# Reordering the work around a convolution in a hybrid layer: next inputs begun earlier, products by turns, residuals at set times, weight sums on another engine

## Chip, cores and metric

One core of one Trainium2 chip. The metric is the device time of the core in microseconds (us); lower is better. The kernel before took 3203.71 us (median of 4 runs).

## The reference

Two layers on x of 4 x 128 x 64 x 64 (four images, 128 channels on the 128 partitions, 4096 pixels), all in float32. The change touches layer 0 only:

```python
def _L0_conv_ref(x, w7, b7, w5, b5, w3, b3, gw, gb, tw, tb, pw, pb, ow, ob):
    x7 = conv2d(x, w7, b7, 3)
    x5 = conv2d(x, w5, b5, 2)
    x3 = conv2d(x, w3, b3, 1)
    xn = nonlocal_block(x, gw, gb, tw, tb, pw, pb, ow, ob)   # softmax attention over the 4096 pixels
    return jax.nn.relu(x7 + x5 + x3 + xn + x)

x = x + _L0_conv_ref(_gn(x), ...)                            # layer 0
# layer 1: a two-way state-space model, then a recurrence, both over the same 4 x 4096 tokens (not touched)
```

## The kernel before

The three convolutions are summed into one 7x7 kernel and done in a transformed (Winograd-like) form: eight products m = 0 to 7 for an image, each with its own transformed input rows ("forms", made on GpSimd) and its own transformed weights (made in turn 0, kept in DRAM, fetched when wanted). The products m = 6, 7 are light (two groups of input, no weights to fetch), m = 1 to 4 have three groups, m = 0, 5 have five. Attention of an image has eight query blocks of 512. So an image is eight *turns*, each of one attention part (scores on TensorE, exp on ScalarE, values on TensorE, the softmax sum `es` on VectorE) and one product; layer 0 has 32 turns, n = 0 to 31. The results of m = 1 to 4 go to four phases of the image rows, so m = 2 and m = 4 leave scaled additions, the *residuals*, to be done in the attention part of a later turn.

```python
# cuts are marked ...
def products(f, kxs):
    pm = ps_c.tile([P, 2, KB // 2 * PC], F32, tag="c", name="pm")     # ring of THREE PSUM tiles, tag "c"
    ...
def put_middle(n, u, v, at):                                          # residuals of m = 2, 4
    spare = lambda: wk.tile([P, 2, KB // 2 * PC], F32, tag="xr", name="sc")        # two tiles
    later(lambda: put(n, 2, u, at * at, spare() if (b, n, 2) in begun else None))  # ScalarE mul, GpSimd add
    later(lambda: put(n, 1, in_(v), at, spare() if (b, n, 1) in begun else None))
    later(lambda: put(n, 3, in_(v), at * at * at, v))
def divide(n, acc, es):
    den = ps_c.tile([P, NC], F32, tag="c", name="den")                # from the same ring
    nc.tensor.matmul(den, k.ones, es[:, 0, :], start=True, stop=True)
    nc.vector.reciprocal(att, den)
    ...
    nc.vector.tensor_tensor(att, acc, att, ALU.mult)
def collect(n, att):                                                  # attention result into the image t
    pc = ps_c.tile([P, NC], F32, tag="c", name="pc")
    nc.tensor.matmul(pc, ow, att, start=True, stop=True)
    nc.vector.tensor_tensor(r, r, pc, ALU.add)
# in weights(): the sums of the kernels, and the "thirds"
nc.gpsimd.tensor_tensor(w[:, z0:z1, 2:5, :], w[:, z0:z1, 2:5, :], w3[:, z0 - 2 : z1 - 2], ALU.add)
nc.gpsimd.tensor_tensor(ac, v[0], v[2], ALU.add)
nc.gpsimd.tensor_tensor(new, ac, v[1], ALU.subtract)
nc.gpsimd.tensor_tensor(v[1], ac, v[1], ALU.add)
# the store of a set of weights
nc.gpsimd.tensor_tensor(both, *own, ALU.add)

FIRST = (6, 7, 1, 2, 0, 5, 3, 4)      # image 0
ORDER = (1, 2, 0, 6, 7, 5, 3, 4)      # images 1, 2
LAST  = (1, 2, 3, 4, 6, 7, 5, 0)      # image 3
for n in range(N):
    b, q = divmod(n, NQ)
    m = (FIRST if b == 0 else ORDER if b + 1 < B else LAST)[q]
    making_forms = forms(m, f)                       # inputs of THIS turn's product
    next(making_forms, None)
    for i in range(NB):                              # attention, 8 pieces
        exs = nxt
        if i + 1 < NB: nxt = scores(th, i + 1)
        values(i, exs, acc, es)
        next(making_forms, None)
        next(making, None)                           # weights, in the first turns
        if m < 6 and i == NB - 3: wts = [fetch(m, 0), fetch(m, 1)]
        if late: late.pop(0)()                       # one residual a piece, as soon as there is one
    for i, _ in enumerate(convolve(b, m, f, wts)):   # half products: first, second, first, ...
        if i == 0:
            ...collects...
            if q == 0 and n: finish(b - 1)           # relu and residual of the whole image b - 1, late too
            atts[n] = divide(n, acc, es)
        if i == 2 and n + 1 < N: th = queries(n + 1) # from the ring "c" as well
    if n + 1 < N: nxt = scores(th, 0)
```

The order of instructions on TensorE and ScalarE is the program's; on VectorE and GpSimd a scheduler sets it at build time. In the traces each engine takes its instructions in that order: in turn 4 of this kernel exp stands behind a residual for which ScalarE waits 14.71 us.

## Time and profile before

| | before |
|---|---|
| median, us | 3203.71 |
| span of the profiled run | 3197.6 |
| to the first values matmul | 39.6 |
| 31 turns (values of turn 0 to values of turn 31) | 1626.4 |
| the rest (turn 31, state-space model, recurrence) | 1531.6 |
| turns 0 / 4 / 8 / 16 / 24 | 77.2 / 74.9 / 58.6 / 59.9 / 59.0 |

A turn's length is read from TensorE's timeline: from its first values matmul to the next turn's.

### The profile page before, as it was taken

The numbers are of one execution on the slowest core, as the hardware profiler recorded it, in microseconds if no ns is written. First come the engines' busy times: TensorE is split into PE (matmuls) and PEld (weight loads), VectorE is DVE, ScalarE is ACT, GpSimd is POOL, SyncE is SP. The second block draws the span as 40 slices with busy tenths as digits, with TensorE's granted clock in tenths as the row PEclk, the third lists the DMA queues.
The fourth block names the chain that finished last, engine by engine and source line by source line (L and its number), as shares of the span: only waits on it lengthen the run. The fifth ranks groups of instructions, "written<-read, shape, count | busy, mean of one in ns | idle before, by whom it ended". The sixth has DMA issues, their size and how long they took to land. (4 is left out here: it accounts for less than half of the span.)

```text
span 3197.6 us, 42890 instructions
## 1 busy us (share of the span) xinstructions
PE 2953.9 (92%) x15511; PEld 1463.8 (46%) x15511; DVE 2263.5 (71%) x3408; ACT 1817.2 (57%) x3102; POOL 1875.5 (59%) x1415
## 2 busy tenths in 40 slices
PE   5798998999989999999997899999999999999986
PEld 1344443445444544344454454544444444444545
DVE  5885676866867677677765676768676767677667
ACT  2343434433435334443443887887788778888756
POOL 6175757825768347677464355556655665555554
PEclk9999999999999999999998899999999999999988
DMA  4310010100111000111003333333433343333332
GB/s 166 144 38 30 23 45 29 62 4 23 38 37 57 8 23 23 38 56 45 1 23 113 93 105 107 91 97 83 116 97 93 91 112 95 97 101 94 88 114 107
DMA packets 108394, 224.16 MB, mean 70 GB/s; under 512 B 25678, under 2 KB 29390, under 8 KB 106764
## 3 DMA queue, kind: packets, MB, share of 16 engines
q1 hardware_dynamic: 96588, 177.53, 19.2%
q10 hardware_dynamic: 11584, 43.78, 3.9%
q8 instruction: 125, 2.05, 0.3%
q14 instruction: 97, 0.79, 0.1%
HBM read 200.83 MB, written 20.44 MB: 69 GB/s over the span
## 5 line engine op out<-in xcount | busy, mean ns | idle before, releaser
L475 DVE TENSOR_TENSOR es<-es,ex 128x1024 f32<-128x1024 f32 x448 | 767.3, 1713 | 121.6 <-ACT ex L460 82.5
L460 ACT ACTIVATE ex<-pf 128x1024 f32<-128x1024 f32 x512 | 502.0, 1023 | 436.9 <-PE pf L458 356.4
L458 PE MATMUL pf<-theta,phi 64*128 64x512 f32 x2048 | 517.9, 623 | 46.0 <-ACT ex L460 44.5
L469 PE MATMUL acc<-ex,gT 128*64 128x512 f32 x2048 | 492.2, 606 | 2.1 <-ACT ex L460 2.1
L1189 POOL TENSOR_TENSOR ct<-ct,Cst 128x512 f32<-128x512 f32 x128 | 169.7, 1326 | 393.1 <-DMA ct<-csmem 332.9
L458 PEld LDWEIGHTS pf<-theta,phi 64*128 64x128 f32 x2048 | 172.8, 187 | 369.8 <-ACT ex L460 226.3
L408 ACT ACTIVATE eo<-pm 128x256 f32<-128x256 f32 x88 | 33.7, 383 | 491.0 <-PE pm L366 491.0
L1155 ACT ACTIVATE lt<-lt,cs 128x128 f32<-128x128 f32 x1024 | 312.1, 390 | 0.3 <-DMA lt<-csmem 0.3
L366 PE MATMUL pm<-yf,wt 128*128 128x256 f32 x1152 | 294.5, 389 | 17.3 <-DVE t L491 12.9
L469 PEld LDWEIGHTS acc<-ex,gT 128*64 128x64 f32 x2048 | 127.6, 137 | 341.0 <-issue 329.4
L366 PEld LDWEIGHTS pm<-yf,wt 128*128 128x128 f32 x1152 | 217.1, 193 | 95.2 <-issue 40.8
L337 POOL TENSOR_TENSOR yf<-yd 128x272 f32<-128x272 f32 x192 | 242.0, 1291 | 0.0
L1090 PE MATMUL pb<-tl,wbc_fwd 128*64 128x512 f32 x512 | 234.9, 602 | 3.2 <-DVE xT L1122 3.2
L1090 PE MATMUL pb<-tl,wbc_bwd 128*64 128x512 f32 x512 | 235.5, 602 | 0.0
L424 POOL TENSOR_TENSOR eo<-eo 128x512 f32<-128x512 f32 x48 | 63.2, 1316 | 271.2 <-DVE eo L418 188.6
L1254 POOL TENSOR_TENSOR yT<-yT,zT 128x512 f32<-128x512 f32 x127 | 171.1, 1355 | 36.9 <-DVE yT L1241 32.4
L1188 DVE TENSOR_TENSOR lt<-lt,gm 128x1024 f32<-128x1024 f32 x128 | 179.7, 1404 | 1.9
L387 POOL TENSOR_TENSOR t<-t,eo 128x512 f32<-128x512 f32 x36 | 50.2, 1394 | 202.5 <-DVE eo L416 201.2
L337 POOL TENSOR_TENSOR yf<-yx 128x272 f32<-128x272 f32 x96 | 151.3, 1604 | 1.6
L1122 DVE SCALAR_TENSOR_TENSOR xT<-px,taps_bwd,xT 128x512 f32<-128x512 f32 x192 | 143.8, 749 | 8.9 <-ACT xT L1116 4.0
L1221 PE MATMUL y<-lt,xdt 128*64 128x128 f32 x2048 | 142.8, 282 | 4.1 <-PE ptr L1164 3.7
L412 DVE SCALAR_TENSOR_TENSOR eo<-pm,eo 128x256 f32<-128x256 f32 x176 | 73.6, 418 | 100.2 <-ACT eo L408 98.1
(297 smaller groups left out, 5792.7 us busy)
## 6 DMA issues: line engine op xcount, KB each, us to landing
lt<-csmem SPq DMA_DIRECT2D x128, 512.0 KB, 5.6
wt<-wd ACTq DMA_DIRECT2D x72, 576.0 KB, 3.7
ct<-csmem SPq DMA_DIRECT2D x256, 128.0 KB, 5.2
rs<-m SPq DMA_DIRECT2D x31, 512.0 KB, 3.6
wd<-t SPq DMA_DIRECT2D x16, 576.0 KB, 3.8
t<-in_x SPq DMA_DIRECT2D x4, 2048.0 KB, 10.9
rows<-after SPq DMA_DIRECT2D x32, 256.0 KB, 4.9
out<-t SPq DMA_DIRECT2D x4, 2048.0 KB, 14.4
```

The source lines that it names most:

```text
L337: nc.gpsimd.tensor_tensor(f[:, kx], at(x), at(y), op)
L366: nc.tensor.matmul(pm[:, e, :], wt, src, start=(i == 0), stop=(i == len(terms) - 1))
L458: nc.tensor.matmul(pf[:, e, :], phi[HALF[e], m, :], th[HALF[e]], start=True, stop=True)
L460: nc.scalar.activation(ex, pf, AF.Exp, scale=scale)
L469: nc.tensor.matmul(acc[HALF[e]], gT[:, 2 * m + e, :], ex[:, e, :], start=(m == 0), stop=(m == NT // 2 - 1))
L475: nc.vector.tensor_tensor(es, es, ex, ALU.add)
L1090: nc.tensor.matmul(out, w[i]["bc"][:, tap, bass.ts(c, DS)], src, start=(tap == 0), stop=(tap == KC - 1),)
L1122: nc.vector.scalar_tensor_tensor(at(n), px, taps[:, PAD - n : KC - n], at(n), ALU.mult, ALU.add)
L1155: nc.scalar.activation(v, v, AF.Relu, scale=-1.0, bias=m["b"]["cs"][:, d, m["i"], h : h + 1])
L1188: nc.vector.tensor_tensor(lt, lt, gm.unsqueeze(2).to_broadcast([P, ND, NHEAD, P]), ALU.mult)
L1189: nc.gpsimd.tensor_tensor(m["ct"], m["ct"], Cs[:, cols].unsqueeze(1).to_broadcast([P, NHEAD, P]), ALU.mult)
L1254: eng.tensor_tensor(v, v, gr["z"][d][:, :, half(d, j // 2)], ALU.mult)
```

## The change

Its intent is to take the waits out of TensorE's way in layer 0. No arithmetic is added or removed. The diff, cut to its core:

```diff
@@ forms
             out.append([both(yx[:, 0:KB], 1)])
+            yield
@@ put_middle: residuals get a turn, and two more spare tiles
-            def put_middle(n, u, v, at):
-                spare = lambda: wk.tile([P, 2, KB // 2 * PC], F32, tag="xr", name="sc")
-                later(lambda: put(n, 2, u, at * at, spare() if (b, n, 2) in begun else None))
+            def put_middle(n, u, v, at, when, own=None):
+                tag = "u" if m == 2 and n == 2 else "xr"
+                spare = lambda: wk.tile([P, 2, KB // 2 * PC], F32, tag=tag, name="sc")
+                later(when, lambda: put(n, 2, u, at * at, own or (spare() if (b, n, 2) in begun else None)))
 ...   (mid tiles: bufs 1 -> 2)
-                    put_middle(n, out, mid[n], U)                 # m = 2
+                    put_middle(n, out, mid[n], U, now + 1)
-                    put_middle(n, in_(u), mid[n], V)              # m = 4
+                    put_middle(n, in_(u), mid[n], V, now + 2, u)
@@ finish
-                later(part, q)
+                later((b + 1) * NQ + 4, part, q)
@@ weights: sums and thirds
-                nc.gpsimd.tensor_tensor(...)      # four lines
+                nc.vector.tensor_tensor(...)
@@ order
-        ORDER = (1, 2, 0, 6, 7, 5, 3, 4)
+        ORDER = (1, 2, 6, 0, 7, 5, 3, 4)
@@ the loop
-            making_forms = forms(m, f)            # at the start of turn n
-            next(making_forms, None)
+                if i == 2 and n + 1 < N:          # in the product of turn n, for turn n + 1
+                    nf = []
+                    making_forms = forms(product(n + 1), nf)
+                    next(making_forms, None)
-                if late:
-                    late.pop(0)()
+                due = late.get(n, [])
+                for _ in range(-(-len(due) // (NB - i))):
+                    due.pop(0)()
-                    atts[n] = divide(n, acc, es)  # at i == 0
+                if i == 1:
+                    atts[n] = divide(n, acc, es)
 ...   (the statistics that layer 1 needs of the finished first image: from turn NQ + 1 to NQ + 5)
```

## The prediction

> **What bounds the kernel now.** I read in this order: the page's 40 slices, the waits of TensorE in the convolution stage, busy times turn by turn, then timelines around the long gaps.
>
> ```profile
> PE   5798998999989999999997899999999999999986
> PEclk9999999999999999999998899999999999999988
> ```
>
> Each slice is 80 us. The convolution and attention stage (layer 0) fills slices 0 to 21, to about 1740 us. The rest (the state-space layer and the recurrence) is not in the diff; I leave its time as it is. Layer 0 runs 32 turns, four images of eight. A turn is an attention part (scores, exp, values for one block of 512 queries: 26.3 us when undisturbed) and then one product of the transformed convolution: light (m = 6, 7) about 12 us, heavy about 16 (m = 1 to 4) or 24 to 26 (m = 0, 5), the first scores of the next turn (4.2 us) not counted. PE is nearly full, so only its idle gaps can be won. The busy times by stretch show how much that is (columns: stretch, its length, then busy us of PE, PEld, DVE, ACT, POOL, then granted clock); these are all 32 turns but the first:
>
> ```profile
> 116.77:1692.00 1575.23, 1502.47 (x6263) 704.93 (x6261) 1140.03 (x1013) 647.32 (x764) 979.60 (x663) 0.99 0.09 33
> ```
>
> That is 73 us idle; the first turn has 30 more (46.8 busy of 77.0) and a clock of 0.84. All that the change can reach is thus near 103 us, 3% of the whole, plus some 14 us of slow clock after gaps. What PE waited for, 40 to 1740 us (total us, times, longest):
>
> ```profile
> PE pf L458 <- ACT ex L460: 44.2, 43, 12.4
> PE den L479 <- DVE es L644: 22.1, 10, 9.7
> PE pm L366 <- DVE t L491: 12.9, 3, 4.8
> PE den L479 <- DVE eo L412: 5.5, 3, 1.8
> PE pm L366 <- DMA wt<-wd: 4.4, 9, 1.6
> ```
>
> Three places hold most of it. **Turn 0**: exp stands still because VectorE does, and VectorE waits for weight sums on GpSimd (first line); the five softmax sums after it then run beside GpSimd's stores of the weights at 3.1 us each (second line):
>
> ```profile
> 55.23 2.63 DVE L576 SCALAR_TENSOR_TENSOR t<-t 128x1152 f32<-128x1152 f32 x2 [14.94 <-POOL t L549]
> 66.33 15.61 DVE L475 TENSOR_TENSOR es<-es,ex 128x1024 f32<-128x1024 f32 x5
> ```
>
> **Turn 4** (m = 0): ScalarE wants a third spare tile for a residual; GpSimd, busy with 26 us of the product's inputs, frees the first only then. Exp queues behind it and PE stands still for 12 us, after which the clock is 0.77 for 12 us more:
>
> ```profile
> 282.21 0.67 ACT L384 ACTIVATE sc<-t 128x512 f32<-128x512 f32 x1 [14.71 <-POOL t L387]
> 272.00:284.00 12.00, 0.15 (x2) 0.15 (x2) 1.95 (x2) 1.78 (x3) 12.00 (x16) 0.66 0.00 0
> 284.00:296.00 12.00, 12.00 (x41) 3.66 (x42) 9.48 (x7) 5.79 (x7) 2.29 (x2) 0.77 0.26 98
> ```
>
> **Turns 8, 16, 24** (m = 1, first of an image): the late residuals of the last image come behind the inputs on GpSimd, the attention result can't be added before them, and its PSUM tile blocks the next product. The matmuls after it run at half speed (3.50 us for eight, elsewhere 1.89):
>
> ```profile
> 534.24 0.69 DVE L491 TENSOR_TENSOR t<-t,pc 128x512 f32<-128x512 f32 x1 [7.15 <-POOL t L387]
> 534.98 3.50 PE L366 MATMUL pm<-yf,wt 128*128 128x256 f32 x8 [4.85 <-DVE t L491]
> ```
>
> **What the Trainium skill says.** "SBUF — State Buffer", section "Who interferes with whom": a VectorE instruction with two SBUF inputs contends with a GpSimd instruction that reads SBUF. The trace agrees: the sum over ex takes 1.22 us where GpSimd is idle, 3.1 us beside the weight stores, 1.71 us on average. "TensorE: Matmul & The Clock Gate", Part 1: after an idle window of about 3.4 us the array runs at half clock until it has been busy as long again. The trace agrees: gaps of 12.0 and 4.85 us are followed by slow matmuls, turns with single gaps of 1.2 to 1.9 us stay at 1.00. "VectorE: DVE Perf Modes", "First, the fixed hardware budget": a reciprocal is an iterative divide with a repeat count of 8[...]. The trace has 3.35 us for 128x512, against 0.67 for a multiply of the size.
>
> **The change part by part.**
>
> *Weight sums on VectorE.* Gone from GpSimd: 15 sums of 128x384 at 0.99 and six of 128x128 at 0.45 to 0.95, 19 us. On VectorE I size them from its rows 128x640 = 1.10, 128x256 = 0.42, 128x128 = 0.29: 15 x 0.55 + 6 x 0.29 = 10 us. The instruction order of the changed kernel has VectorE begin them at about 31, wait for the first exp at 38.5, and do 9.6 us of them, so the first softmax sum comes at 49.5 instead of 59.1, and the first pair operation at 53.0 instead of 55.2. From there both kernels have the same 12 pair operations (1.35 each) beside the same weight stores, and the changed one has two softmax sums fewer left. I get the end of VectorE's sums at 96.7 instead of 101.9: **5 us**. TensorE gains 2.6 more there, as it does a product half before the denominator. Turn 0: -7 (77 to 70). It stays bound by VectorE.
>
> *Residuals in a chosen turn, four spare tiles instead of two.* Turn 4's ScalarE never waits for a spare tile now. In the new order GpSimd does the four residual additions after 33 us of inputs and sums that begin at 244, so by about 283, when the attention results (after 281) want them: little or no wait. -12 gap, -4 slow clock: -16.
>
> *Residuals of m = 4 two turns on, the finish of an image four turns later.* Turns 8, 16, 24 lose the wait for t. They took 58.7, 59.9 and 59.1. Without gaps: 46.0 (PE busy in turn 9, same heavy form) + 0.4 (a collect more, a transpose group less) + 1.4 (usual small waits for exp) + 1.05 (the new gap, last part) = 48.9. -9.8, -11.0, -10.2: -31.
>
> *Inputs from the middle of the product before on.* GpSimd starts them some 12 us earlier. In the steady turns they were not late (no PE wait for yf in the list), so this pays only in the turns above, by leaving less GpSimd work beside VectorE's sums. Nothing more counted.
>
> *Heavy and light by turns* (order 1,2,6,0,7,5,3,4): sums stay the same; no gain counted.
>
> *The denominator a step later* (the divide after the second half of the first product). The waits of den for es and eo outside the turns already counted are 0.95 + 1.88 + 1.22 + 1.21 + 1.30 + 3 x 1.84 = 12, and go: -12. Turn 26 also loses 1 us of a wait for exp: -1. But the PSUM ring of products has three tiles. Before, the third allocation after den came 4.3 us or more after it; now it is the second product's second half, after den's issue (0.86), four products (1.72) and the query projection (0.86). From den's start: it could begin at 3.44, its tile is free at 1.02 + 0.05 + 3.35 + 0.08 = 4.50. **A new PE gap of 1.05 us** in each turn whose middle product has one form: all but m = 0 and 5, with the three turns that also make keys 27 in place of 24 + 3; less one in turn 0 and three in 8, 16, 24, where I have counted it: 23 x 1.05 = +24.
>
> Sum: -7 - 16 - 31 - 12 - 1 + 24 = -43. A few us may come from softmax sums less slowed by GpSimd (ScalarE waited 38 us for them outside turn 0, little of it reached PE): -4. 3202.45 - 47 = **3155**.
>
> **The rivals.**
> 1. *The reciprocal's gap does not appear or costs little.* Against: the round of three tiles, and in turn 8 the query projection already waited for att in this trace. If PE's queue hid it: -24 more, 3131, faster by 2.2%.
> 2. *VectorE is let off in turn 0 more than I think.* Its 34 us excess over an undisturbed turn is the largest single item. If the weight stores no longer met the sums: -12 more. For: the stores start about 1 us earlier only, so I don't believe it.
> 3. *GpSimd's new order makes a new wait.* Inputs of the next product now stand before additions of the current one, and collects wait for additions into the image. GpSimd is 62% busy from 117 to 1692 (979.6 of 1575), so a queue would drain within a turn. If turn 4 keeps half its gap and the m = 1 turns 3 us each: 3155 + 8 + 9 = 3172.
> 4. *All off the path, as PE is full*: 3200. Against: the gaps above are PE's own.
>
> **Range and chances.** 3131 (rival 1) and 3172 (rival 3) are one-sided departures, and a few us come from slow clock either way. 8 in 10: 3128 to 3180. Faster by over 2% means under 3138.4, so it takes rival 1 or 2 nearly whole: 0.2. Slower by 2% would take 107 us, and nothing here makes that: 0.02. Within: 0.78.
>
> **What would show it.** Right: a new line "PE pm <- DVE att" of 20 to 28 us in some 24 to 27 waits of about 1 us; the waits of den near zero outside turn 0; no PE gap over 2 us in turns 4, 8, 16, 24, and clock 1.00 there; turn 0 about 70 us long and VectorE's wait of 14.94 gone; the start of the state-space layer some 45 us earlier and its length the same. Wrong: PE waiting for yf or for t with GpSimd behind; the spare tile still waited for; turn 0 under 60 or over 77 us; or no waits for att, and a time near 3130.

## The result

3147.19 us (median of 4 runs, 3143.78 to 3148.85) against 3203.71: ratio 0.9824, 95% interval 0.9807 to 0.9841. It was run again: 3146.45, ratio 0.9834 (0.9820 to 0.9847). A ratio here is the mean time of one kernel's runs over that of the other's in the same rounds, so it is not quite the ratio of the medians quoted. The gain is 1.8% (1.7% the second time).

| turn lengths from the traces, us | before | after | predicted change | measured change |
|---|---|---|---|---|
| turn 0 | 77.2 | 68.5 | -7 | -8.7 |
| turn 4 | 74.9 | 63.3 | -16 | -11.6 |
| turns 8, 16, 24 together | 177.5 | 143.2 | -31 | -34.3 |
| the other 26 | 1296.8 | 1299.0 | +7 | +2.2 |
| 31 turns | 1626.4 | 1574.0 | -47 | -52.4 |
| the rest | 1531.6 | 1530.3 | 0 | -1.3 |

The page after, TensorE's two rows of the 40 slices (78.6 us each now):

```profile
PE   6899999999999999999997999999999999999976
PEclk9999999999999999999998999999999999999988
```

The dents of turns 4, 8 and 16 are gone. The busy times of the stretch that holds all turns but the first (its length, then busy us of PE, PEld, DVE, ACT, POOL, granted clock) answer to the 73 us idle of before:

```profile
108.40:1613.90 1505.50, 1461.97 (x6152) 691.95 (x6150) 1053.92 (x1005) 632.45 (x751) 916.24 (x662) 1.00 0.10 34
```

1505.5 less 1462.0 leaves 43.5 us idle, at full clock but for 3.4 us in turn 12. What TensorE waited for from 40 to 1690 us (total us, times, longest):

```profile
PE pf L460 <- ACT ex L462: 19.6, 39, 2.2
PE pm L367 <- DVE att L483: 16.1, 19, 0.8
PE den L481 <- DVE es L651: 11.0, 1, 11.0
...
PE den L481 <- DVE eo L414: 0.9, 1, 0.9
```

Three things are to be seen. The waits for exp fell from 44.2 to 19.6 and have no long one. The denominator waits once only, in turn 0. And a wait that was not there before has come: 19 times 0.85 us for `att`, the result of the reciprocal. This is one of them, in turn 8 (start, length, engine, line):

```profile
504.75 1.02 PE L481 MATMUL den<-es,ones 128*128 128x512 f32 x2
...
505.81 3.36 DVE L483 RECIPROCAL att<-den 128x512 f32<-128x512 f32 x1 [0.17 <-PE den L481]
...
507.33 1.04 PE L449 MATMUL pt<-xp,tw 128*128 128x512 f32 x2
...
509.22 1.13 PE L367 MATMUL pm<-yf,wt 128*128 128x256 f32 x4 [0.85 <-DVE att L483]
```

The product at 509.22 is the third tile after `den` in a ring of three. It starts 4.47 us after `den`; without the reciprocal it could have started 3.44 after it, since TensorE's issue of two 512-column matmuls takes 0.86. The loss is thus 1.03 us, of which the profile draws 0.85 as idle, because it draws a matmul on to its modelled end.

VectorE in turn 0 after:

```profile
49.22 1.22 DVE L477 TENSOR_TENSOR es<-es,ex 128x1024 f32<-128x1024 f32 x1
...
52.54 2.63 DVE L578 SCALAR_TENSOR_TENSOR t<-t 128x1152 f32<-128x1152 f32 x2
...
64.70 11.98 DVE L477 TENSOR_TENSOR es<-es,ex 128x1024 f32<-128x1024 f32 x4
...
79.19 2.63 DVE L578 SCALAR_TENSOR_TENSOR t<-t 128x1152 f32<-128x1152 f32 x2 [2.51 <-POOL t L571]
```

The wait of 14.94 us for GpSimd is gone. But four softmax sums still take 11.98 us instead of 4.9, beside the weight stores on GpSimd (the view merges them: one took 1.21 us, three about 3.5), and at 79.19 VectorE waits 2.51 us for a store's addition to end.

### The profile page after: what moved, and what is told of

Read it like the earlier page. It is cut to its first block, busy times and chain, and to the rows that moved or that the text cites.

```text
span 3144.2 us, 42863 instructions
## 1 busy us (share of the span) xinstructions
PE 2939.4 (93%) x15511; PEld 1459.0 (46%) x15511; DVE 2198.3 (70%) x3429; ACT 1815.3 (58%) x3102; POOL 1799.3 (57%) x1394
## 5 line engine op out<-in xcount | busy, mean ns | idle before, releaser
L477 DVE TENSOR_TENSOR es<-es,ex 128x1024 f32<-128x1024 f32 x448 | 684.2, 1527 | 137.6 <-ACT ex L462 104.5
L367 PE MATMUL pm<-yf,wt 128*128 128x256 f32 x1152 | 287.1, 382 | 12.2 <-DVE att L483 11.0
L337 POOL TENSOR_TENSOR yf<-yd 128x272 f32<-128x272 f32 x192 | 234.1, 1247 | 1.4
L337 POOL TENSOR_TENSOR yf<-xp 128x272 f32<-128x272 f32 x128 | 109.7, 889 | 133.3 <-PE pm L367 127.5
L1103 PEld LDWEIGHTS pb<-tl,wbc_fwd 128*64 128x64 f32 x512 | 65.5, 138 | 164.3 <-issue 137.1
L367 PE MATMUL pm<-yf,wc 128*128 128x256 f32 x512 | 131.5, 385 | 6.6 <-DVE att L483 5.1
## 6 DMA issues: line engine op xcount, KB each, us to landing
t<-in_x SPq DMA_DIRECT2D x4, 2048.0 KB, 10.8
```

The costliest lines, as they stand in the source:

```text
L337: nc.gpsimd.tensor_tensor(f[:, kx], at(x), at(y), op)
L367: nc.tensor.matmul(pm[:, e, :], wt, src, start=(i == 0), stop=(i == len(terms) - 1))
L477: nc.vector.tensor_tensor(es, es, ex, ALU.add)
L1103: nc.tensor.matmul(out, w[i]["bc"][:, tap, bass.ts(c, DS)], src, start=(tap == 0), stop=(tap == KC - 1),)
```

## The experiments

Eleven kernels ran in three groups; each gave the reference's result. "31 turns" is read from the traces, as in the table above; the median and the ratio to the kernel before (of the same group) are of the timed runs.

| run | 31 turns | the rest | median | ratio, 95% interval |
|---|---|---|---|---|
| before | 1626.4 | 1531.6 | 3203.71 | |
| the change | 1574.0 | 1530.3 | 3147.19 | 0.9824 (0.9807 to 0.9841) |
| the change again | 1576.0 | 1527.5 | 3146.45 | 0.9834 (0.9820 to 0.9847) |
| 1 divide early | 1569.0 | 1534.9 | 3141.83 | 0.9814 (0.9795 to 0.9832) |
| 2 inputs late | 1583.9 | 1529.8 | 3157.96 | 0.9877 (0.9858 to 0.9897) |
| 3 two spare tiles | 1580.6 | 1530.8 | 3151.43 | 0.9847 (0.9831 to 0.9864) |
| 4 sums on GpSimd | 1580.2 | 1530.1 | 3156.06 | 0.9867 (0.9851 to 0.9884) |
| 5 old order | 1581.2 | 1531.3 | 3155.02 | 0.9854 (0.9827 to 0.9880) |
| 6 residuals only | 1597.9 | 1535.6 | 3169.32 | 0.9900 (0.9877 to 0.9923) |
| 7 stores on VectorE | 1565.8 | 1526.8 | 3140.84 | 0.9819 (0.9796 to 0.9841) |
| 8 queries later | 1567.7 | 1536.0 | 3141.39 | 0.9815 (0.9794 to 0.9837) |
| 9 first image light | 1573.3 | 1536.9 | 3147.06 | 0.9828 (0.9815 to 0.9841) |
| 10 three edits | 1557.1 | 1532.7 | 3130.21 | 0.9777 (0.9763 to 0.9790) |

"The rest" is nearly all code that every one of these kernels shares, and it varies from 1526.8 to 1536.9, by 2.8 us between two traces of one kernel. So the totals of 1, 3, 5, 7, 8 and 9, whose intervals overlap the change's, can't be told from it; what is said of them rests on the turns. The kernel before had medians of 3197.89, 3200.17 and 3200.98 in the three groups, so across groups the ratios are to be compared, not the medians.

**1. Divide early.** The change with the divide back at i == 0.

```diff
-                if i == 1:
-                    atts[n] = divide(n, acc, es)
+                    atts[n] = divide(n, acc, es)   # in the block of i == 0
```

> The changed kernel with the divide put back to the first step of a convolution (denominator before the second half of the first product). My theory: the 19 TensorE gaps of 0.85 us before the product that reuses the denominator's PSUM tile vanish (16 us), and waits of the denominator for the softmax sum come back, but fewer than the 17 us of before since VectorE lags less: 5 to 10 us, turn 0 of them 2 to 3. So 3138 to 3142 us against 3147, ratio to before 0.980. Rival (moving the divide was a gain): the waits of the denominator come back with 20 us or more and the time is 3150 or higher.

Measured: no wait for att is left. TensorE's waits for the denominator from 40 to 1690 us:

```profile
PE den L481 <- DVE es L651: 19.4, 5, 13.7
```

Outside turn 0 (13.7 of it) that is 5.7 us. The 31 turns are 5.0 us shorter than the change's, though turn 0 is 1.7 and turn 4 is 2.2 longer. So in this kernel the move of the divide, taken alone, costs time: it was worth 18 us of waits in the kernel before (22.1 and 5.5, less the 9.7 of turn 0), but with the other parts in place 5.7 us of them are left to win, less than the 19 gaps cost. The total (ratio 0.9814) is too coarse to show 5 us.

**2. Inputs late.** The change with the inputs begun at the start of their own turn again.

```diff
-                if i == 2 and n + 1 < N:
-                    nf = []
-                    making_forms = forms(product(n + 1), nf)
-                    next(making_forms, None)
+            making_forms = forms(m, f)             # at the start of turn n
+            next(making_forms, None)
```

> The changed kernel with the inputs of a product again begun at the start of its own turn. My theory: in the steady turns they are not late, so all turns but 4, 8, 16, 24 stay within 0.5 us, turn 4 grows by 4 to 8 us, since its residual additions come later on GpSimd and the attention results wait for them, and 8, 16, 24 by about 1 us each: 3152 to 3158. Rival 1 (this is the part that made the gain): turns 8, 16, 24 go back by more than 5 us each and the time is above 3165. Rival 2 (it costs nothing): 3147.

Measured: turn 4 grows by 6.2 us, turns 8, 16 and 24 by 1.7 each, turn 26 by 2.8; turns 12 and 28 shrink by 2.4 and 1.1; the rest within 0.5. (That 12, 26 and 28 move is outside my theory.) In turn 4 TensorE now waits as my theory says, for an attention result that can't be added before the residuals on GpSimd are:

```profile
PE pc L491 <- DVE t L493: 6.6, 1, 6.6
```

The 31 turns are 9.9 us longer. So this part is worth 10 us, in few turns, where I had counted nothing for it on its own.

**3. Two spare tiles.**

```diff
-                tag = "u" if m == 2 and n == 2 else "xr"
+                tag = "xr"
```

> The changed kernel with two spare tiles for scaled residuals instead of four (the m = 2 residual of the second half takes the same tag as the first). It differs only in turn 4, the one turn where all four are wanted. My theory: ScalarE waits there for GpSimd again, behind the inputs of m = 0, and turn 4 grows from 63 by 8 to 12 us; no other turn changes: 3155 to 3159. Rival (the earlier inputs alone had freed turn 4): turn 4 within 1 us and 3147.

Measured: turn 4 69.8 us, 6.6 more; every other turn within 0.25. ScalarE waits for the third spare tile, as before the change, though for 10.8 us instead of 14.7:

```profile
270.53 0.67 ACT L385 ACTIVATE sc<-t 128x512 f32<-128x512 f32 x1 [10.78 <-POOL t L388]
```

The mechanism is right; the size is below the 8 to 12 expected, since ScalarE waits a part of that time in the change as well (experiment 5).

**4. Sums on GpSimd.** The four `nc.vector` lines of sums and thirds as `nc.gpsimd` again.

> The changed kernel with the weight sums and thirds back on GpSimd. My theory: only turn 0 changes; VectorE waits for GpSimd before its first pair operation again, turn 0 grows by 5 to 8 us from 68.5: 3152 to 3155. Rival (turn 0 is bound by the weight stores beside the softmax sums, and the sums' engine does not matter): turn 0 within 2 us and 3147.

Measured: turn 0 75.5 us, 7.1 more; turn 1 0.6 less; all others the same to 0.2. VectorE's wait is back:

```profile
55.56 2.62 DVE L578 SCALAR_TENSOR_TENSOR t<-t 128x1152 f32<-128x1152 f32 x2 [14.96 <-POOL t L551]
```

**5. Old order.** `ORDER = (1, 2, 0, 6, 7, 5, 3, 4)` in the change.

> The changed kernel with the old order of products in the middle images (1, 2, 0, 6, 7, 5, 3, 4). My theory: the order is worth nothing by itself, since GpSimd drains within a turn and the residual of m = 2 is then only ScalarE work: turns 10 and 11, and 18 and 19, keep their sums (99.3 and 100.3 us) within 2 us: 3146 to 3151. Rival (a heavy product right after m = 2 makes the inputs late): those pairs grow by 4 us or more each: 3155 or higher.

Measured: my theory fell. Turns 18 and 19 together take 105.8 us instead of 100.3 (turns 10 and 11, 101.2 instead of 99.4, stay within its 2 us); the 31 turns are 7.2 us longer. TensorE stands still for 3.88 us in turn 18, with 3.4 us of half clock after it, and for 1.72 us in turn 10. In turn 18 ScalarE stands for 6.8 us before a residual. ScalarE's line, then GpSimd's ahead of it:

```profile
993.51 0.67 ACT L385 ACTIVATE t<-t 128x512 f32<-128x512 f32 x1 [6.79 <-POOL t L432]
```

```profile
977.53 6.39 POOL L337 TENSOR_TENSOR yf<-yd 128x272 f32<-128x272 f32 x4
983.88 3.83 POOL L337 TENSOR_TENSOR yf<-xp 128x272 f32<-128x272 f32 x3
987.67 2.14 POOL L347 TENSOR_TENSOR yd<-yx 128x560 f32<-128x560 f32 x1
...
992.20 1.27 POOL L432 TENSOR_TENSOR t<-eo 128x512 f32<-128x512 f32 x1
```

L432 is the sum of m = 1 and m = 2 in turn 17, which the residual scales. It now lies behind the inputs of the next product, which the change begins earlier. A heavy product's inputs hold it up past the time when ScalarE wants it, and exp waits behind. A light one's do not: in the change the second L432 of turn 17 begins at 970.89 instead of 992.20, and ScalarE's residual at 973.84 waits for nothing. So the order is the counterpart of the earlier inputs: it keeps them from making a new wait. That the old order costs little without them is seen in experiment 6, which has the old order and the late inputs: there turns 18 and 19 take 100.2 us, 10 and 11 99.3.

The same wait is left in turn 4 of the change, where image 0 has m = 0 after m = 2 (ScalarE's line, the change):

```profile
264.47 0.66 ACT L385 ACTIVATE sc<-t 128x512 f32<-128x512 f32 x1 [4.68 <-POOL t L432]
```

**6. Residuals only.** The kernel before with the times of residuals and finish changed, four spare tiles, two mid tiles, and the later statistics of layer 1 that go with the later finish; nothing else of the diff.

> The kernel before with only the timing of the residuals and of the finish changed (and the spare and middle tiles that this needs); inputs, order, divide and weight sums as before. My theory: this part alone makes turns 8, 16, 24 short (from 59 to some 50 us) and takes 3 to 5 us from turn 4, which keeps a gap for want of earlier inputs; turn 0 stays at 77: 33 us less, 3166 to 3174, ratio 0.989 to 0.991. Rival (the parts only work together): turns 8, 16, 24 above 55 us, ratio above 0.994.

Measured: turns 8, 16, 24 take 50.5, 50.7 and 50.7 us, turn 4 70.1, turn 0 80.0 (2.8 more, not the 77 expected); the 31 turns are 28.5 us shorter than before's 1626.4. More than half of the gain (28.5 of 52.4) is this part, and it needs none of the others.

**7. Stores on VectorE.** The additions that go with the weight stores.

```diff
-                nc.gpsimd.tensor_tensor(both, *own, ALU.add)
+                nc.vector.tensor_tensor(both, *own, ALU.add)
```

> The changed kernel with the six additions that go with the weight stores on VectorE too. It moves 6 x 1.35 = 8 us of work onto the engine that binds turn 0. My theory (the softmax sums are slow there because GpSimd reads beside them, 3.1 against 1.2 us): about seven sums get 1.9 us shorter each, 13 us, so turn 0 falls by 4 to 6 us from 68.5: 3140 to 3143. Rival (VectorE is bound by its own amount of work): turn 0 grows by 6 to 8 us: 3153 to 3155.

Measured: turn 0 61.5 us, 7.0 less than in the change, though VectorE has six more instructions in it. Every softmax sum of the turn takes 1.22 us now, and a store's addition 1.35 (GpSimd took 4.8 each for the first two):

```profile
64.91 1.35 DVE L571 TENSOR_TENSOR ws<-t 128x1152 f32<-128x1152 f32 x1
66.18 1.22 DVE L477 TENSOR_TENSOR es<-es,ex 128x1024 f32<-128x1024 f32 x1
```

The rival (VectorE's amount of work) would have made turn 0 longer. What bound turn 0 in the change is VectorE held up by the stores on GpSimd. That is not the slow sums alone: three sums of about 3.5 us and the last one (L651, 2.98 us against 0.68 here) cost some 9 us, and the wait of 2.51 us for a store's addition is gone too; less 5.4 us for the four additions that VectorE now does before its last sum, this leaves an estimated 6 of the 7.0. No run parts the two.

**8. Queries later.** The ring tile of `den` goes to the query projection in turns of three or more groups; in light turns the divide is at i == 0.

```diff
-                if i == 1:
+                if i == (1 if m < 6 else 0):
                     atts[n] = divide(n, acc, es)
-                if i == 2 and n + 1 < N:
+                if i == (3 if m < 6 and not more else 2) and n + 1 < N:
                     th = queries(n + 1)
```

> The changed kernel with the PSUM tile of the denominator reused later: in heavy turns the query projection comes after the second half of the middle product, so that product takes the tile before it and the projection the denominator's; in light turns the divide is at the first step. My theory (the 0.85 us gaps are the reciprocal holding one of three tiles, and TensorE has no slack): the 19 waits of TensorE for att vanish and each such turn is 0.5 to 0.9 us shorter: 3130 to 3136. Rival (the gap moves into another wait, of the scores for theta or of the denominator): turns stay within 0.3 us and the time at 3147.

Measured: the wait for att is gone from the list. From 110 to 1607 us:

```profile
PE pm L367 <- DMA wt<-wd: 3.3, 9, 0.5
PE den L481 <- DVE es L651: 3.3, 2, 1.9
```

The gap was the ring, then. But it did not all come back: the turns of m = 1 to 4 with a gap are 0.2 to 0.6 us shorter (one, turn 14, 1.2), not 1.03, as TensorE now reaches the third set of weights before they have landed (nine waits of up to 0.5 us, which the gap had hidden). Light turns from 10 on are 0.5 to 1.1 shorter, but for turn 20 (1.5 longer; its statistics matmul waits 2.2 us for VectorE instead of 1.1, and 3.4 us of half clock follow). Turns 0 and 1, light turns in which VectorE lags, are 1.5 us longer each. The 31 turns are 6.3 us shorter, about half of the 11 to 17 expected.

**9. First image light.** `FIRST = (6, 1, 2, 7, 0, 5, 3, 4)`: m = 2 followed by a light product in image 0 too.

> The changed kernel with the first image's products in the order 6, 1, 2, 7, 0, 5, 3, 4, so that its m = 2 too is followed by a light product. My theory (from the old order: ScalarE's residual waits for the combining sum that GpSimd does behind the inputs of a heavy product): turn 4 loses its two gaps and falls from 63.3 by 3 to 4.5 us to about 59.5; turns 1 to 3 keep their sum of 139 within 2 us: 3142 to 3145. Rival (turn 4 is long by its own matmuls): turn 4 within 1 us, 3147.

Measured: the two gaps of turn 4 (1.78 and 1.33 us) are gone, as the finding of experiment 5 says. The turn is 2.2 us shorter and not 3.1, as 3.4 us of half clock fall into it here. But turns 1 to 3, 138.9 us in the change, take 141.5: in turn 1 VectorE has the statistics of another image between the softmax sums (that this is what makes it longer is argued, not shown). The 31 turns are 0.7 us shorter, less than two traces of one kernel differ; nothing is won.

**The change again** ran beside 9 and 10:

> The changed kernel again, unaltered, as the anchor of this group. Turns within 0.3 us of the first trace (turn 0 within 1 us); its state-space part may differ by some 4 us from the first trace's 1530, as it did among kernels that share its code: 3144 to 3150, ratio 0.981 to 0.984.

Measured: 26 turns within 0.3 us of the first trace; turns 1, 4, 5, 12 and 13 differ by 0.7 to 0.9, outside what was expected; the 31 turns are 2.0 us longer. "The rest" is 2.8 us shorter.

**10. Three edits together** (7, 9, and 8 with the divide at i == 1 also in the light turns of image 0).

> The changed kernel with three edits together: the first image's order as in the run before, the additions of the weight stores on VectorE, and the denominator's tile reused by the query projection in heavy turns, with the divide at the first step in light turns after the first image. If they add: 3.5 + 7 (turn 0, measured alone) + about 8 (the turns from 2 on where the late query projection gained, measured alone): 18 us less, 3126 to 3132, ratio 0.976 to 0.978. Rival (they meet in turns 0 to 4 and in part cancel): 3136 to 3142.

Measured: 3130.21 us, ratio 0.9777 (0.9763 to 0.9790), clear of the change run beside it (0.9834, 0.9820 to 0.9847). Its 31 turns are 16.9 us shorter than the change's first trace (18 were expected if the parts add). It beats both kernels by the times.

## Why the prediction was right

The time was foretold as 3155, the range as 3128 to 3180; it came to 3147.2. The change in the 31 turns was foretold as -47 us and was -52.4. By its steps:

- *The three places.* Right: turns 0, 4, 8, 16 and 24 lost 54.6 us together, and nothing else much.
- *Turn 0: -7.* Right in mechanism and size (-8.7; experiment 4 puts 7.1 on the sums). The first softmax sum was foretold for 49.5 and came at 49.22, the first pair operation for 53.0 and came at 52.54, the end of the sums for 96.7 and came at 94.45. Rival 2, that the weight stores no longer meet the sums, did not happen in the change; made to happen (experiment 7) it was worth 7.0 us, not the 12 estimated.
- *Turn 4: -16.* Mis-sized, -11.6. The spare tile was no longer waited for, as foretold. The step that failed is "little or no wait": ScalarE waited 4.68 us for the sum of m = 1 and m = 2, which the earlier inputs had pushed back on GpSimd (TensorE idle for 1.78), and the collects waited once more (1.33). These are 3.1 of the 4.4 us that are missing. The other 1.2 are the slow clock, sized at 4 us where the line shown, 0.77 over 12 us, gives 2.8. That is rival 3 in one turn and at a smaller size.
- *Turns 8, 16, 24: -31.* Right, -34.3. Experiment 6 shows that it is the time of the residuals and the finish: with them alone the turns fall to 50.5 to 50.7.
- *The denominator: -12, then +24.* The waits went, all but 0.9 us outside turn 0. The new gap came, with the tile named and a size of 1.03 us for a foretold 1.05. Its count was wrong: 24 turns have a product of one form, and I added the three with keys to them again, though they are among the 24. In those three the transpose waits for ScalarE instead, and turns 0 and 28 wait for theta. So 19 gaps, 20 us, in place of the 28 in the sum. Rival 1 (no gap) is out.
- *Inputs earlier: nothing more counted.* Wrong by itself: 9.9 us (experiment 2), 6.2 of them in turn 4, where I had put them under the residuals. Against that it made the waits of experiment 5.
- *Heavy and light by turns: no gain counted.* Wrong once inputs are early: 7.2 us (experiment 5). "A queue would drain within a turn" is true of GpSimd's mean load, but what counted was one sum in the queue and when ScalarE wanted it.

That the sum came so near is in part luck. The gain was underrated in turn 0, in turns 8, 16, 24 and in the others (by 1.7, 3.3 and 4.8 us) and overrated in turn 4 (by 4.4); and two effects that the prediction did not see, the wait that earlier inputs make behind m = 2 and the order that takes it away, cancel each other. Some of its readings are off without weight: the sums "at 3.1 us each" beside the stores are one of 1.22 and four of about 3.5 (last section), 2% slower would have taken about 111 us and not 107, and it starts from one run (3202.45) and not from the median of four.

What each part is worth is not additive: undoing one at a time costs 9.9 (inputs), 7.2 (order), 6.6 (spare tiles, part of the residuals), 6.2 (sums) and -5.0 (divide); residuals alone give 28.5.

Open: why "the rest" differs by up to 10 us between traces of kernels that share its code. The first waits of the state-space model differ (the wait of its first matmuls for GpSimd's scaled rows was 2.9 us in the change, 5.4 in experiment 8), but no run was made for it.

## What to carry to other kernels

Where one engine is full, look turn by turn for its gaps and for the queue behind each; a residual or a finish that may come at any time should come where the queue is short, and such a move, with the tiles it needs, gave half of this gain alone. When work is begun earlier on an in-order engine, ask what now lies behind it and who wants that next: the order of products is what made the earlier start safe. In a ring of tiles count how many allocations after a slow reader its tile comes round again; moving the reader one step made 19 gaps here.

## What the Trainium skill lacked or had wrong

- "SBUF — State Buffer", "Who interferes with whom", lacked nothing for turn 0. It calls what VectorE and GpSimd share an exclusive lock, and says that the order of issue and not the kind of operation decides who waits. The trace agrees. From turn 0 of the kernel before, each instruction from a window of its own, since the view merges neighbours (spans on GpSimd are rough):

```profile
63.92 1.22 DVE L475 TENSOR_TENSOR es<-es,ex 128x1024 f32<-128x1024 f32 x1
64.09 6.02 POOL L569 TENSOR_TENSOR ws<-t 128x1152 f32<-128x1152 f32 x1 [8.89 <-DVE t L578]
65.06 1.35 DVE L580 SCALAR_TENSOR_TENSOR t<-t 128x1152 f32<-128x1152 f32 x1
66.33 1.22 DVE L475 TENSOR_TENSOR es<-es,ex 128x1024 f32<-128x1024 f32 x1
67.65 3.54 DVE L475 TENSOR_TENSOR es<-es,ex 128x1024 f32<-128x1024 f32 x1
```

  A pair operation and a sum that follow on VectorE without a pause take 1.35 and 1.22 us inside the store, as alone, and it is the store that is long (6.02 us; 2.75 for the one at 78.11). After VectorE's first pause, 0.10 us at 67.55, the next sum takes 3.54 us and ends 1.08 after the store (70.11).

- "VectorE: DVE Perf Modes", "First, the fixed hardware budget", says how a reciprocal is made but not how long it takes: 3.35 us for 128x512 float32, five times a multiply of that size. That number decided whether a ring of three tiles was enough.
- "TensorE: Matmul & The Clock Gate", Part 1, gives an idle window of about 3.4 us before the clock is halved (what it says of frequent short idles names no length). Long gaps fit (one of 3.88 us, in turn 18 of experiment 5, was followed by 0.84 over the next 10.8 us). But here 3.4 us of half clock also began within 1.5 us of the end of gaps of 1.11 us (turn 24 of the kernel before), 1.46 and 1.98 (turns 12 and 0 of the change) and 2.42 (turn 16 before), while 2.43 in turn 8 before left the clock at 1.00. The gap of 1.58 us in turn 4 was followed by it in one trace of the change and not in the other, so the length of a gap did not decide alone; the cause is open. After that gap, the change again and then its first trace (stretch, length, busy us of PE, PEld, DVE, ACT, POOL, granted clock):

```profile
307.34:310.75 3.41, 3.41 (x11) 0.69 (x10) 2.67 (x3) 2.05 (x2) 3.41 (x3) 0.50 0.00 0
309.70:313.10 3.40, 3.40 (x17) 1.02 (x16) 2.90 (x3) 1.94 (x2) 3.40 (x3) 1.00 0.00 0
```
